# ScalarE multiplies more of a slot table's rows; three PSUM bank strings and the order of the first stage's steps change

## The chip, the cores and the metric

The kernel runs on one core of a Trainium2 chip. The metric is the device time of one execution in microseconds, the median of several runs. The engines of the core work side by side, each through its own queue in order: PE (TensorE: matmuls and transposes), ACT (ScalarE: activations and copies), DVE (VectorE), POOL (GpSimd) and SP (SyncE, which issues most of the DMAs). PE writes its results to PSUM, which here is eight banks of 128 x 512 f32. A bank can be written again only when the engine that reads it has read it.

## What is computed

The input x is 8 batches of 512 tokens with 512 features. Two branches read the same layernorm of it, and their product is added to x:

```python
xn = _layernorm(x, axis=-1)
s = _L0_attn_ref(xn, Wq, Wk, Wv, Wo, Wg1, Wg2, norm_weight)
g = _silu(_L0_ffn_ref(xn, gate_w, Wg, Wu, Wd, sWg, sWu, sWd, shared_gate_w))
x = x + s * g
```

The first branch is linear attention with a decay, 16 heads of 32, in chunks of 128 tokens:

```python
q = silu(xn @ Wq); k = silu(xn @ Wk); v = xn @ Wv        # by heads
q, k = rotate(q), rotate(k)
scores = einsum('bthd,bshd->bhts', qi, ki) * D           # in a chunk
o_inter = einsum('bthd,bhde->bthe', qi * decay_q, S)     # the chunks before
S = lam_C * S + einsum('bshd,bshe->bhde', ki * decay_k, vi)
o = group_rmsnorm((o_intra + o_inter) * sigmoid(xn @ Wg1 @ Wg2)) * norm_weight
s = o @ Wo
```

The second is a mixture of 16 experts (512 to 128 to 512, SwiGLU). The router picks four of them for each of the 4096 tokens and scales their softmax weights to a sum of one. A shared expert, the same for all tokens, is added under a sigmoid gate.

## The kernel before

**Stages.** By the trace: to about 200 us the first stage, in which every batch is normed, transposed, routed and sent through the shared expert, a piece at a time (`first`, a generator), between the parts of batch 0's attention. From 200 to 226 the tokens are sorted by expert (`sort`) while PE ends batch 0's attention. From 226 to 284 the slot table is made (`table`), between the parts of batch 1's attention. From 304 to 693 the expert blocks run over gathered tokens, at full PE. From 693 on come the attention of batches 2 to 7 and the mixture of all parts into the output.

**PSUM.** `bank(tag, name)` (L115) gives one of four rings: "a" of four banks, "k" and "m" of one each, "d" of two. Keys (`key`, a product with wk and then Silu on ACT, L669) take "m", queries "d". The values (`value`, L615, copied by ACT at L619) take "m" for even tiles and "d" for odd ones. Scores (`scores`, L725) take all four of "a", which DVE empties by multiplying with a mask (L750). The state products (L714) lie in "k".

**The first stage's pieces for a batch**, in order: route_1 (plT, "a"), share_1 (pg in "m", read by Silu, and pu in "d"), then norm of a later batch and turn of the next (psT, four transposes to "a", copied by ACT at L291), route_2 (pl, a transpose to "a"), and share_2, whose four row tiles pys_b_t take the banks of a string, are copied by ACT (L374) and stored. Names in the trace carry the batch and tile: pys_2_0 is batch 2's first row tile. The stores and loads of x, the two halves of xn_d (L262, L275) and xT_d go through SP's queue. `along` is the step that `sequence(0, ...)` calls: each call runs one or two such pieces (nine fifths on average).

**A group of four heads** in `sequence(b, step, ...)`: scores of group g, a step, the key product of group g + 2 (or a value tile of the next batch, where there is no such group), the transpose of the next group's keys (by_token, L691, then ACT's kd at L696), a step, the query of g + 2, the output (po, L766 and L772, multiplied into on by DVE, L776), a step. Behind the first group's query stands the second half of the gate (gate_2, tiles p at L645), four "a" banks read by ACT's Sigmoid into on (L649). gate_2 runs at this place for batches 0 and 1 only. For batch 0 the step is `along`. For batch 1 it does nothing, and the table's parts are called from within products instead (between[0], after each of the four matmuls).

**The slot table.** `sort` has given each of the 128 lists (a rank and a tile of tokens) its places. The lists are taken in eight groups of 16 (GROUP). For a group, make(i) writes two one-hot arrays in two halves of eight lists each: place (L526, 128x512 f16) and block (L529, 128x2288 f16). The row of a list in place is then multiplied by the tokens' numbers: for the first eight lists of a group by one DVE instruction (L533, with half_token), for the other eight by number(), one ACT instruction for each list (L542, 128x64 f16). Sixteen matmuls (pn, L565, an "a" bank) multiply place with block, and DVE adds the result up (L574; the first is a cast, L576). Two homes for place and block alternate between groups. number(i + GROUP, ...) is called in three parts, of lists 0 to 4, 5 to 9 and 10 to 15, the first before and the others behind the matmuls of group i.

**Order.** Each engine's order is fixed when the kernel is built. Matmuls are issued in the order of the program; the instructions of ACT and DVE stand in their queues as a scheduler of the build has placed them.

Of the kernel before, what the change touches and what calls it, by code (L numbers as in the profile page):

```python
# [47 lines left out]
GROUP = 16  # L48
# [49 lines left out]
def tile_block(ctx: ExitStack, tc: tile.TileContext, a: dict, out: bass.AP):  # L98
# [8 lines left out]
    def bank(tag, name):  # L107
        return pp.tile([P, 512], F32, tag=tag, name=name, bufs={"a": 4, "k": 1, "m": 1, "d": 2}[tag])
# [255 lines left out]
    def share_2(b):  # L364
        h = h1_of.pop(b)
        xT1_of.pop(b)
        for t in range(NC):
            sh = p1.tile([P, D], F32, tag="sh1", name=f"sh1_{b}_{t}", bufs=6)
            py = bank("dama"[t], f"pys_{b}_{t}")
            with on_pe():  # L370
                nc.tensor.matmul(
                    py, lhsT=h[:, t * P : (t + 1) * P], rhs=sw[:, KC * 2 * F :],
                    start=True, stop=True)
            nc.scalar.copy(sh, py)  # L374
            nc.sync.dma_start(sh_d[b][t * P : (t + 1) * P, :], sh)
# [110 lines left out]
    def table(room):  # L486

        half = room.bitcast(F16)  # L490
        free = [0]
        quads = GROUP // QUAD


        def part(*shape):
            n = int(np.prod(shape))
            free[0] += n
            flat = half[:, free[0] - n : free[0]]
            return flat.rearrange("p (q j) -> p q j", j=QUAD) if len(shape) == 2 else (
                flat.rearrange("p (u q j) -> p u q j", u=quads, j=QUAD))  # L500

        homes = [(part(quads, HALF, QUAD), part(quads, 2 * NB, QUAD))]
        free[0] = 2 * WE * (LATE - LATE // 2)
        homes.append((part(quads, HALF, QUAD), part(quads, 2 * NB, QUAD)))

        def flat(n):
            free[0] += n
            return half[:, free[0] - n : free[0]]

        acc = flat(2 * NB)  # L510

        def rows(of, n):
            return of.rearrange("p (u j) -> p u j", j=QUAD).unsqueeze(2).to_broadcast(
                [P, of.shape[-1] // QUAD, n, QUAD])

        def make(i):
            place, block = homes[i // GROUP % 2]
            for u in range(0, quads, quads // 2):
                us = slice(u, u + quads // 2)
                lists = slice(i + u * QUAD, i + (u + quads // 2) * QUAD)  # L520

                def counts(n):
                    return count[:, :n].unsqueeze(1).to_broadcast([P, quads // 2, n, QUAD])

                with tc.issue_after(masked[0]) if i == GROUP and u == 0 else nullcontext():
                    nc.vector.tensor_tensor(  # L526
                        place[:, us], counts(HALF), rows(sp[:, 0, lists], HALF), ALU.is_equal)
                with tc.issue_after(masked[0]) if i == GROUP and u == 0 else nullcontext():
                    nc.vector.tensor_tensor(  # L529
                        block[:, us], counts(2 * NB), rows(sp[:, 1, lists], 2 * NB),  # L530
                        ALU.is_equal)
                if u == 0:
                    nc.vector.tensor_tensor(  # L533
                        place[:, us], place[:, us], rows(half_token[:, lists.start % NT :][
                            :, : GROUP // 2], HALF), ALU.mult)

        def number(i, some):
            place = homes[i // GROUP % 2][0]
            for j in range(max(some[0], GROUP // 2), some[1]):
                row = place[:, j // QUAD, :, j % QUAD]  # L540
                t = (i + j) % NT
                nc.scalar.activation(row, row, AF.Copy, scale=token[:, t : t + 1])  # L542

        yield
        make(0)
        for j in range(0, GROUP, 4):
            number(0, (j, j + 4))
            yield
        for i in range(0, TOPK * NT, GROUP):
            more = i + GROUP < TOPK * NT  # L550
            if more:
                make(i + GROUP)
            else:
                for e in range(E - LATE, E - LATE // 2):
                    nc.sync.dma_start(wexp[:, e, :], a["experts"][:, e, :])
            if i < TOPK * NT // 2:
                yield
            place, block = homes[i // GROUP % 2]
            pn = bank("a", f"pn_{i}")
            for some in ((0, 5), (5, 10), (10, GROUP)):  # L560
                if some[0] == 5:
                    with on_pe():
                        for j in range(GROUP):
                            h = j % 2 * HALF
                            nc.tensor.matmul(  # L565
                                pn[h : h + HALF, : 2 * NB],
                                lhsT=place[:, j // QUAD, :, j % QUAD],
                                rhs=block[:, j // QUAD, :, j % QUAD], start=(j < 2),
                                stop=(j >= GROUP - 2))
                if more:  # L570
                    number(i + GROUP, some)
                if some[1] == GROUP:
                    if i:
                        nc.vector.tensor_tensor(acc, acc, pn[:, : 2 * NB], ALU.add)  # L574
                    else:
                        nc.vector.tensor_copy(acc, pn[:, : 2 * NB])  # L576
                yield
        pt = bank("a", "pslot")
        with on_pe():
            for h in range(2):  # L580
                nc.tensor.matmul(
                    pt[h * HALF : (h + 1) * HALF, :NB], lhsT=fold,
                    rhs=acc.rearrange("p (b h) -> p b h", h=2)[:, :, h], start=True, stop=True)
        t = const.tile([P, NB], I32, tag="slot", name="slot")
        with behind(DVE):
            nc.vector.tensor_scalar(t, pt[:, :NB], float(B * N // 2), None, ALU.add)
        slots.append(t)
# [90 lines left out]
    def key(b, g, ps=None):  # L678
        kT_of[g] = rotated(b, g, "k", wk, ps)
# [177 lines left out]
    def sequence(b, step, projected, before=None, defer=False, also=lambda: None):  # L857


        n = b + 1  # L860

        def project_tiles(q, ts):
            if q is not None:
                for t in ts:
                    projected(q, t, project(q, t))


        fill = ([0], [1], [2], [3], [], [], [], [])
        for g in range(G):
            scores(b, g)  # L870
            step()
            if g + 2 < G:
                key(b, g + 2)
            else:
                value(n, 2 * (g - 2))
            if g + 1 < G:
                by_token(b, g + 1)
            project_tiles(before, fill[2 * g])
            step()
            if g + 2 < G:  # L880
                query(b, g + 2)
                if g + 3 == G and n not in xT_of:
                    load_xT(n)
            if g + 2 == G:
                value(n, 1)
            if g == 0 and b not in on_of:
                gate_2(b)
            project_tiles(before, fill[2 * g + 1])
            if fill[2 * g + 1] == [NC - 1]:
                on_of.pop(before, None)  # L890
            output(b, g)
            if defer and g + 2 == G:
                gate_1(n)
            step()
        v_of.pop(b)
        if n == FIRST:
            for _ in range(4):
                next(filling)
            gate_1(n)
            next(filling, None)  # L900
            for e in range(E - LATE // 2, E):
                nc.sync.dma_start(wexp[:, e, :], a["experts"][:, e, :])
            squares(b)
            inverse(b)
            value(n, 3)
            normed(b)
            experts_of_blocks()
            return
        if defer:
            gate_2(n)  # L910
        value(n, 3)
        also()
        squares(b)
        step()
        inverse(b)
        key(n, 0)
        also()
        query(n, 0)
        normed(b)
        also()  # L920
        if not defer:
            step()
        key(n, 1)
        by_token(n, 0)
        if defer:
            step()
        query(n, 1)
        also()
        if not defer:
            gate_1(n)  # L930
            project_tiles(b, [0, 1])
            also()
            project_tiles(b, [2, 3])
            also()
            on_of.pop(b)
        step()
# [556 lines left out]
```

## Time and profile before

| | us |
|---|---|
| median of three runs | 1140.58 (1140.27 to 1141.29) |
| the profiled execution | 1134.81 |
| its span in the trace | 1133.0 |
| first stage, to about 200: PE busy | 188.72 of 200.00 |
| table, 226 to 284: PE, DVE, ACT busy | 53.57, 55.51, 30.81 of 58.00 |
| blocks, 304 to 693: PE busy | 389.00 of 389.00 |
| 693 to 1133: PE busy | 429.92 of 440.00 |

The span is the time from the first to the last instruction of the profiled execution; all places in the trace are given in microseconds from its start. A line of a timeline has the start, the duration of a run of like instructions, the engine, the line of the kernel, the operation, and out<-in. A remark in brackets gives the idle time of the engine before it and what ended it. A line of the list of waits has what waited, for what, and then the total, the number and the longest of such waits.

### The profile page before, as it was taken

To read this page: it belongs to the slowest core of one execution; us is meant where nothing else is said; L and a number is where in the kernel's file an instruction comes from. 1 tells how busy PE (TensorE), PEld (TensorE's weight loads), DVE (VectorE), ACT (ScalarE), POOL (GpSimd) and SP (SyncE) were. 2 spreads that over 40 slices of the span, in tenths; PEclk is the share of its full clock that TensorE was granted. 3 is DMA by queue.
4 is the path that set the end of the run, shared out by engine and by line. 5 is a ranking of instruction groups with operands and counts; after the bars stand their busy time and mean duration, and the time that the engine had idled before them with its cause. 6 is when DMAs were issued, how large, how long until landed. Compare 5 with 4: busy or idle time off the path is not lost. (4 is left out here: it accounts for less than half of the span.)

```text
span 1133.0 us, 21299 instructions
## 1 busy us (share of the span) xinstructions
PE 1106.5 (98%) x7670; PEld 675.5 (60%) x7670; DVE 737.3 (65%) x1584; ACT 428.6 (38%) x924; POOL 447.2 (39%) x430
## 2 busy tenths in 40 slices
PE   7999999998999999999999999999999999999998
PEld 4445554455577777777777775655645555546453
DVE  6357744899344455444445446968889597797774
ACT  3223424264443333333333442353442522523541
POOL 4212100200333333333333323855877858858211
PEclk9999999999999999999999999999999999999999
DMA  9995342092789999989999975824647537444012
GB/s 341 326 319 191 143 151 48 22 383 70 239 201 234 244 236 241 240 237 239 237 240 249 256 204 216 292 81 142 232 121 236 177 113 258 143 136 142 19 38 75
DMA packets 163930, 218.48 MB, mean 193 GB/s; under 512 B 89840, under 2 KB 99184, under 8 KB 161776
## 3 DMA queue, kind: packets, MB, share of 16 engines
q1 hardware_dynamic: 142704, 146.76, 41.6%
q0 software_dynamic: 21120, 70.34, 23.4%
q8 instruction: 63, 1.03, 0.4%
q14 instruction: 43, 0.35, 0.1%
HBM read 126.78 MB, written 72.43 MB: 176 GB/s over the span
## 5 line engine op out<-in xcount | busy, mean ns | idle before, releaser
L1224 PE MATMUL pgu<-xts,wst 128*128 128x256 f32 x896 | 202.6, 379 | 0.0
L1224 PEld LDWEIGHTS pgu<-xts,wst 128*128 128x128 f32 x896 | 170.1, 190 | 46.2 <-issue 13.2
L1343 POOL DMA_INDIRECT yg<-y_d,place x128 | 142.8, 1115 | 30.3 <-issue 18.3
L1153 POOL DMA_INDIRECT more<-xn_d,slot x69 | 65.6, 951 | 216.6 <-DVE w L1207 113.8
L1255 PE MATMUL py<-wexp,slb 128*128 x272 | 129.9, 593 | 0.0
L1259 DVE TENSOR_SCALAR y<-py,w 128x512 f32<-128x512 f32 x136 | 102.0, 750 | 41.5 <-PE py L1255 34.8
L615 PE MATMUL pv<-wv,xT 128*128 128x512 f32 x256 | 118.2, 602 | 1.0 <-ACT sh L374 1.0
L659 PE MATMUL pk<-xT,wk 128*128 128x512 f32 x256 | 118.2, 603 | 0.0
L659 PE MATMUL pq<-xT,wq 128*128 128x512 f32 x256 | 115.7, 593 | 0.3 <-PEq L1307 0.3
L1236 ACT ACTIVATE slb<-pgu 128x256 f32<-128x256 f32 (+1 forms) x80 | 28.2, 352 | 222.7 <-PE pgu L1224 180.6
L1237 DVE TENSOR_TENSOR slb<-slb,pgu 128x256 f32<-128x256 f32 (+1 forms) x80 | 30.5, 381 | 121.1 <-ACT slb L1236 121.1
L817 PE MATMUL pw<-wo,on 128*128 128x512 f32 x224 | 100.6, 596 | 5.2 <-DVE m L1381 4.4
L1153 POOL DMA_INDIRECT xg<-xn_d,slot x67 | 63.7, 950 | 101.4 <-DVE w L1207 48.2
L1385 POOL TENSOR_TENSOR xo<-xo,m 128x512 f32<-128x512 f32 x31 | 45.3, 1462 | 128.1 <-DVE m L1381 120.9
L1186 ACT COPY xts<-pl 128x512 uint16<-128x512 uint16 x110 | 84.3, 769 | 2.4 <-DMA pl<-more 1.3
L750 DVE TENSOR_TENSOR sc<-ps,dmask 128x512 f32<-128x512 f32 x128 | 79.0, 676 | 1.0 <-PE ps L725 1.0
L659 PEld LDWEIGHTS pq<-xT,wq 128*128 128x128 f32 x256 | 47.2, 190 | 54.2 <-issue 52.7
L615 PEld LDWEIGHTS pv<-wv,xT 128*128 128x128 f32 x256 | 46.0, 190 | 51.3 <-issue 46.8
L659 PEld LDWEIGHTS pk<-xT,wk 128*128 128x128 f32 x256 | 46.2, 189 | 50.7 <-issue 48.3
L817 PEld LDWEIGHTS pw<-wo,on 128*128 128x128 f32 x224 | 41.2, 190 | 54.5 <-issue 45.2
L1205 DVE COPY wst<-wexp 128x512 f32 x112 | 43.2, 426 | 37.0 <-DVE y L1259 15.7
L1255 PEld LDWEIGHTS py<-wexp,slb 128*128 128x128 f32 x272 | 45.5, 191 | 27.4 <-issue 26.8
(196 smaller groups left out, 1713.1 us busy)
## 6 DMA issues: line engine op xcount, KB each, us to landing
y_d<-y SPq DMA_DIRECT2D x136, 256.0 KB, 4.1
wexp<-in_experts SPq DMA_DIRECT2D x16, 768.0 KB, 5.0
sh_d<-sh SPq DMA_DIRECT2D x32, 256.0 KB, 3.5
xT<-xT_d SPq DMA_DIRECT2D x8, 1024.0 KB, 6.7
m<-sh_d SPq DMA_DIRECT2D x32, 256.0 KB, 4.6
xo<-in_x SPq DMA_DIRECT2D x32, 256.0 KB, 2.8
out<-xo SPq DMA_DIRECT2D x31, 256.0 KB, 2.0
x<-in_x SPq DMA_DIRECT2D x7, 1024.0 KB, 8.8
```

The lines of the kernel that those rows point to most:

```text
L615: nc.tensor.matmul(pv, lhsT=xT_of[b][:, k, t * P : (t + 1) * P], rhs=wv[:, k, :], start=(k == 0), stop=(k == KC - 1))
L659: nc.tensor.matmul(ps, lhsT=w[:, k, g * P : (g + 1) * P], rhs=xT_of[b][:, k, :], start=(k == 0), stop=(k == KC - 1))
L750: masked[:] = [nc.vector.tensor_tensor(s, pss[j].rearrange("p (c t) -> p c t", t=C), dmask[:, g * HG + j].unsqueeze(1).to_broadcast([P, NC ...
L817: nc.tensor.matmul(pw, lhsT=on_of[b][:, g, t * P : (t + 1) * P], rhs=wo[:, g, :], start=(g == 0), stop=(g == G - 1))
L1153: nc.gpsimd.indirect_dma_start(out=row(i), out_offset=None, in_=xn_d, in_offset=bass.IndirectOffsetOnAxis(ap=slot[:, i : i + 1], axis=0))
L1186: (nc.vector.tensor_copy if j in by_dve else nc.scalar.copy)(xt[:, u, KP:, :].bitcast(U16).rearrange("p k (t h) -> p h k t", h=2), pls[j % ...
L1205: nc.vector.tensor_copy(to, wflat[:, bass.ds(off + u * KC * F, KC * F)])
L1224: nc.tensor.matmul(pg[:, o * 2 * P : (o + 1) * 2 * P], lhsT=wst[j % 2][k // KP][:, (k % KP * 2 + o) * F :][:, :F], rhs=xt[:, :, k, :], sta ...
L1255: nc.tensor.matmul(py, lhsT=hT[:, u * P : (u + 1) * P], rhs=wflat[:, bass.ds(off + KC * 2 * F, D)], start=True, stop=True)
L1259: gone.append(nc.vector.tensor_scalar(y, py, w[:, u : u + 1], None, ALU.mult).ins)
L1343: nc.gpsimd.indirect_dma_start(out=yg, out_offset=None, in_=y_d, in_offset=bass.IndirectOffsetOnAxis(ap=place[:, r, g : g + 1], axis=0))
L1385: nc.gpsimd.tensor_tensor(xo, xo, m, ALU.add)
```

## The change

- In make(), L533 is now issued for the first half of group 0 alone, and not for each group. In number(), the rows start from list 0 for all groups but the first. So seven DVE instructions of 128x512 go, and 7 x 8 = 56 ACT instructions of 128x64 come.
- share_2 takes the banks "mdaa" for its four row tiles in place of "dama", for all eight batches.
- In sequence, for batch 0, the step behind the scores now stands behind the key product (or value tile). For other batches it stays where it was.
- gate_2 at batch 1's first group takes "aaam", so that its last tile lies in the key's bank. For batch 0 it stays "aaaa".

```diff
@@ share_2
-            py = bank("dama"[t], f"pys_{b}_{t}")
+            py = bank("mdaa"[t], f"pys_{b}_{t}")
@@ table: make, number
-                if u == 0:
+                if i == u == 0:
                     nc.vector.tensor_tensor(
                         place[:, us], place[:, us], rows(half_token[:, lists.start % NT :][
                             :, : GROUP // 2], HALF), ALU.mult)
 
         def number(i, some):
             place = homes[i // GROUP % 2][0]
-            for j in range(max(some[0], GROUP // 2), some[1]):
+            for j in range(max(some[0], 0 if i else GROUP // 2), some[1]):
                 row = place[:, j // QUAD, :, j % QUAD]
                 t = (i + j) % NT
                 nc.scalar.activation(row, row, AF.Copy, scale=token[:, t : t + 1])
@@ sequence
             scores(b, g)
-            step()
+            if b:
+                step()
             if g + 2 < G:
                 key(b, g + 2)
             else:
                 value(n, 2 * (g - 2))
+            if not b:
+                step()
             if g + 1 < G:
                 by_token(b, g + 1)
...
             if g == 0 and b not in on_of:
-                gate_2(b)
+                gate_2(b, banks="aaam" if b else "aaaa")
```

No matmul, no load and no store is added or left out.

## The prediction

> **What bounds the kernel now.** I read the busy shares first, then busy time by stage, then PE's waits, then the timeline of each place where PE waits.
>
> ```profile
> PE 1106.5 (98%) x7670; PEld 675.5 (60%) x7670; DVE 737.3 (65%) x1584; ACT 428.6 (38%) x924; POOL 447.2 (39%) x430
> ```
>
> PE is busy for 1106.5 of 1133.0 us, so a gain can only come from its waits or its work, and its work stays as it was. By stage (PE, PEld, DVE, ACT, POOL, clock, DMA share, GB/s):
>
> ```profile
> 200.00:226.00 26.00, 26.00 (x122) 12.17 (x121) 23.74 (x44) 4.76 (x11) 5.95 (x5) 1.00 0.07 19
> 226.00:284.00 58.00, 53.57 (x730) 31.59 (x732) 55.51 (x103) 30.81 (x97) 0.00 (x0) 1.00 0.61 229
> 304.00:693.00 389.00, 389.00 (x1697) 289.50 (x1695) 187.21 (x478) 153.18 (x301) 123.04 (x130) 1.00 0.92 231
> ```
>
> The slot table is made at 226 to 284, beside batch 1: there DVE is full (55.51 of 58) and PE waits for it. From 304 to 693 PE never pauses, so whatever PE gains or loses earlier is handed on to the end. PE's waits up to 335 us (total, times, longest):
>
> ```profile
> PE psT L289 <- DVE mv L252: 6.9, 1, 6.9
> PE pn L565 <- DVE sc L750: 3.1, 2, 2.3
> PE p L645 <- DVE wexp L576: 1.4, 1, 1.4
> PE psT L289 <- DVE sc L750: 1.0, 1, 1.0
> PE pv L615 <- ACT sh L374: 1.0, 1, 1.0
> PE pg L355 <- ACT sh L374: 0.9, 1, 0.9
> PE pl L318 <- DVE sc L750: 0.8, 1, 0.8
> ```
>
> The 6.9 is the start-up. The others are all that the change can win: some 3.7 us in the first stage, 4.5 in the table stage.
>
> **First stage, what goes.** Listed waits run from a modelled end; the true cost is the start less the start that the order alone would give, which lies 0.1 to 0.17 earlier. pg_2 starts at 55.49, not 54.50: 0.99. psT at 154.97, not 153.86: 1.11. pl_7 at 180.06, not 179.23: 0.83. pv_2 at 184.86, not 183.65: 1.21. Sum 4.14. pg_2 and pv_2 wait because the third shared row tile, before them in the one bank "m", must be copied by ACT; psT and pl_7 wait for scores' "a" banks, which DVE empties by L750, and the step after key or value puts 3.5 us of PE work between. I take all four as gone.
>
> **First stage, what comes.** "m" has one buffer. Each pair of its users that the new order makes adjacent on PE pays a turnaround. The waits show the price:
>
> ```profile
> 184.24 1.06 ACT L374 COPY sh<-pys 128x512 f32<-128x512 f32 x2
> 184.86 1.55 PE L615 MATMUL pv<-wv,xT 128*128 128x512 f32 x3 [1.04 <-ACT sh L374]
> ```
>
> The first copy takes 0.59 (184.24 to 184.83) and PE starts 0.03 later. And in the kernel before, pys_2_0 follows pk_0 at once, because it takes a "d":
>
> ```profile
> 64.32 3.60 PE L659 MATMUL pk<-xT,wk 128*128 128x512 f32 x8
> 67.76 1.45 PE L371 MATMUL pys<-sw,h 128*128 128x512 f32 x3
> 67.96 0.60 ACT L669 ACTIVATE sk<-pk 128x512 f32<-128x512 f32 x1 [2.73 <-PE pk L659]
> ```
>
> With "mdaa" it needs pk_0's own bank: Silu 67.96 + 0.60 + 0.03 = 68.59, not 67.76: 0.83. Reading the new banks along PE's built order I find five such pairs: pk_0 then pys_2_0, pk_2 then pg_4, pk_3 then pg_5 at 0.83 each; pv_2 of batch 0 then pys_1_0 (46.5 us) and pv_2 then pys_7_0 at 0.72, where a transpose (pl, 0.11) lies between. Sum 3.93. Net: 3.93 - 4.14 = -0.2.
>
> **What else the steps' move touches.** On PE it puts pk_2, pk_3, pv_0 and pv_2 ahead of a step each. pv_0 now starts at 153.9 and needs xT_1; its load is issued at 143.55 on SP's queue and lands in 6.7 (median), at 150.3: 3.6 spare, and SP's built order has it earlier, ahead of four stores of hs. SP's other swaps (xn_d stores against loads of x) lie before 100 us, with DMA full; I cost them at nothing since x is loaded steps ahead, and at 0 to 1.0 for the range, by the 1.04 that pv waited. POOL's queue is unchanged. pl_7 now comes behind pv_2: PE at 182.8, the mask's DVE chain from lg to L345 takes 2.9 as before (181.72 to 184.62), so it is ready at 186.1, and ptotal comes at 187.1: cover shrinks from 3.8 to 1.0, and if it goes, ptotal waits for the excess.
>
> **Table stage, what goes and comes.** Seven of eight L533 multiplications leave DVE (0.42 long, 0.34 start to start): 7 x 0.34 = 2.4 at most. ACT takes 56 more L542 rows. Their price by a row: eight back to back in 2.04, 0.24 each, so 13.5 us; by the mean of a single one, 0.353, it is 19.8. I take 0.24, since they come in runs of 5 to 11. The Trainium skill's "VectorE: DVE Perf Modes", section "TRN2 errata — SBUF-src ops pay a fixed extra latency per instruction", says a small SBUF tile pays a fixed bubble, 224 cycles on ScalarE, and to prefer tiles of 512 elements or more. For 64 elements at 1.2 GHz it gives 0.240 as an estimate, the row's step; it speaks against trading 7 wide DVE instructions for 56 narrow ones.
>
> ACT has the time (30.81 + 13.5 of 58), but its queue is in order, and the new rows stand ahead of things PE and DVE wait for:
>
> ```profile
> 237.49 0.60 ACT L669 ACTIVATE sq<-pq 128x512 f32<-128x512 f32 x1 [3.60 <-PE pq L659]
> 238.10 1.28 ACT L649 ACT_TABLE_LOAD   x1
> 240.39 2.07 ACT L649 ACTIVATE on<-p 128x512 f32<-128x512 f32 x4 [1.00 <-PE p L645]
> ```
>
> In the built order five rows stand ahead of sk_2, eight ahead of sq_2, ten between sq_2 and the table load. Following it from 230 us in before's times:
> - The five rows need group 1's first place (L526, 232.83 + 0.42, ready to ACT at 233.29), so sk_2 runs at 234.49 to 235.09, not 232.37; DVE's L671, free at 234.42 without L533, waits 0.71.
> - Group 2's place is ready at 238.1; five rows end at 239.3, sq_2 at 239.9, ten more at 242.3, the table load at 243.6. The four sigmoids (on) run at 243.6 to 245.7, not 240.4 to 242.5.
> - PE's gate matmuls no longer wait for L576 (2.05 by the start). But ps_1 needs the "a" banks that on reads, and "aaam" gives it only the fourth: it starts at 245.25, not 242.47, and pk_3, which needs the fourth's "m", at 246.3:
>
> ```profile
> 242.47 1.19 PE L725 MATMUL ps<-qT,kT 32*128 32x128 f32 x32
> 243.59 2.84 PE L659 MATMUL pk<-xT,wk 128*128 128x512 f32 x6
> ```
>
> - There PE is 2.7 behind. DVE, at L776, waits 1.26 for on; its next place operation waits 0.84 for PE's pn_16; L671 of sk_3 0.15. With the 0.71, DVE waits 2.96 and has saved 6 x 0.34 = 2.04 by then.
> - PE's later waits (pn_48, 0.8; pn_80, 2.3) take most of the 2.7 back: pn_48's goes, pn_80's falls to 1.55. sc_3 ends at 276.95, not 275.91, and pn_112 starts 1.0 later.
>
> Table stage: +1.0. The Trainium skill's "ScalarE: Activation LUTs", section "What ACT_TABLE_LOAD costs", puts a table switch at about 2.66 us with a drain. Here the load takes 1.28 and the next row can follow at once; by the page each of the two loads would put on back by 1.4, and the sum would be +2.4. I go by the row.
>
> Sum: -0.2 + 1.0 = +0.8, all of it passed on at 304: the span 1133.0 becomes 1133.8. The profiled run took 1134.81 and the runs' median is 1140.58, 7.6 above the span; I keep that: 1141.4.
>
> **Rivals.**
> 1. Faster, because ACT keeps up: sk, sq and on come so early against their readers that nothing waits for them, and the 2.4 of DVE time comes off the stage that DVE fills. For it: DVE 55.51 of 58. Against: the chain above, where sk, sq and on each come 2 to 3 us later. -0.2 - 2.4: 1138.0. If also the turnarounds were hidden, -4.14 - 2.4: 1134.0, but nothing on PE lies in those gaps.
> 2. Slower, by one mechanism: on is late and PE's 2.7 at ps_1 isn't won back, because DVE, itself 1 us late, stays the last for pn_80 and sc_3. It decides if pn_80's wait stays at 2.3. Then -0.2 + 2.7 = +2.5: 1143.1; with rows of 0.353, the 23 ahead of on add 23 x 0.11 = 2.6 more: 1145.7. For it: DVE has 2.5 us free in 58. Against: the two waits are on the page.
> 3. The turnarounds alone: as the forecast, but the table stage neutral: 1140.4. It falls within the same band.
>
> **Numbers.** 0.2%, or 2.3 us, is about what a measurement of this kernel can tell from no change: 1138.3 to 1142.9. Forecast with rival 3: 0.52; rival 2: 0.30; rival 1: 0.18. The forecast's own range is 1139.9 to 1142.9 (each stage to 0.8 or so). The range of 8 in 10 takes in rival 1's 1138.0 and most of rival 2, of which it leaves out the end with the dear rows: 1137.8 to 1144.8. Faster 0.18, same 0.52, slower 0.30.
>
> **What would show it.** Right, if PE's list loses pg, psT and pl behind L374 and L750 before 200, and shows five waits of 0.6 to 0.7 by the list for ACT (sk L669, v L619); if on runs some 3 us later against the start of its batch, ps L725 waits for it (about 2.7), and pn's waits shrink. Wrong, if pys and pg start without waiting after pk, if L542's step isn't near 0.24, or if the stretch 226 to 284 holds less PE idle time than 4.4. A change of pace after 304 would mean that I missed a cause altogether.

## The result and the profile after

The changed kernel takes 1142.07 us (median of 12 runs) where the kernel before, run beside it, takes 1138.85: a ratio of 1.0035 (95% interval 1.0023 to 1.0047), slower, and by more than the 0.2% that the forecast took as no change. The forecast's time, 1141.4, is only 0.7 us off, but by luck: it rested on 1140.58 as the time before, 1.7 above the median here, and on a loss of 0.8 us. The loss is 3.2 us by the medians and 4.0 by the ratio.

The busy shares of the changed kernel, and its stages (PE, PEld, DVE, ACT, POOL, clock, DMA share, GB/s):

```profile
PE 1110.8 (98%) x7670; PEld 677.5 (59%) x7670; DVE 738.9 (65%) x1577; ACT 441.2 (39%) x980; POOL 447.0 (39%) x430
```

```profile
200.00:226.00 26.00, 26.00 (x122) 12.17 (x121) 22.73 (x44) 5.28 (x12) 5.94 (x5) 1.00 0.04 14
226.00:284.00 58.00, 53.08 (x595) 29.84 (x595) 51.92 (x93) 38.82 (x139) 0.00 (x0) 0.94 0.56 210
...
304.00:693.00 389.00, 389.00 (x1697) 289.64 (x1695) 187.08 (x485) 154.05 (x302) 124.35 (x132) 1.00 0.94 232
```

DVE did lose work in the table stage and ACT got it. The fixed stretch shows this only roughly, since the table ends later in the changed kernel; over the whole table (227.48 to 283.32 before, 228.69 to 288.93 after) DVE's busy time went from 53.73 to 51.90 us and ACT's from 29.82 to 43.00. PE lost 0.5 us of busy time between 226 and 284, though, and the column before the DMA share differs: the granted clock was 0.94 there, and 1.00 before and after. The blocks are full as before, so nothing was won back. PE's waits:

```profile
PE psT L289 <- DVE mv L252: 7.0, 1, 7.0
PE ps L725 <- ACT on L649: 3.3, 1, 3.3
PE pg L355 <- ACT sk L669: 2.8, 2, 2.0
PE pn L565 <- DVE sc L750: 1.6, 2, 1.4
PE pys L371 <- ACT v L619: 1.1, 2, 0.6
PE pw L817 <- DVE on L810: 0.8, 1, 0.8
PE pys L371 <- ACT sk L669: 0.7, 1, 0.7
```

The four waits of the first stage that the change was to remove are gone, and so is p's for L576. In their place stand pys and pg behind ACT, and one wait of 3.3 us at ps L725.

To compare profiles of different executions I take three places on PE: the first pu matmul (16.13 us in the kernel before; it differs by the start-up), batch 1's first scores (227.48) and pslot, the end of the table (283.32). The first stage is the time from the first to the second, 211.35 us before, and the table from the second to the third, 55.84. The changed kernel has 1.16 more in the first stage and 4.40 more in the table. Kernels whose first stage is as before show -0.13 to -0.15 there, so 0.14 is the play of the start, and the first stage's loss is 1.3.

**First stage.** PE and ACT of the changed kernel around pg_5, the shared product behind pk_3:

```profile
124.84 3.70 PE L659 MATMUL pk<-xT,wk 128*128 128x512 f32 x8
130.57 3.70 PE L355 MATMUL pg<-xT,sw 128*128 128x512 f32 x8 [2.03 <-ACT sk L669]
```

```profile
128.62 1.28 ACT L669 ACT_TABLE_LOAD   x1 [4.92 <-PE pk L659]
129.92 0.60 ACT L669 ACTIVATE sk<-pk 128x512 f32<-128x512 f32 x1
```

pk_3 ends at 128.5. sk_3 is the first Silu after batch 0's sigmoids, so a table load stands ahead of it, and it begins only when pk_3 is there: 1.28, then Silu's 0.60, then pg_5 at 130.57, 0.05 after Silu's end. The turnaround is 2.1 us by the starts, not 0.83. In the kernel before, the first Silu after the sigmoids was sl_5, beside pu_5's matmuls, and its load had ended 3.6 us before pg_5 was there, so it cost PE nothing:

```profile
122.02 1.28 ACT L359 ACT_TABLE_LOAD   x1
126.88 0.60 ACT L359 ACTIVATE sl<-pg 128x512 f32<-128x512 f32 x1 [3.57 <-PE pg L355]
```

ACT stood idle for 4.92 us ahead of sk_3's load too, but this load began only when pk_3 was there, in all six profiles with this order of steps. Why one load runs ahead of its Silu's input and the other doesn't, the runs don't show.

**Table.** ACT, PE and the clock in the changed kernel (columns of the last as above):

```profile
240.51 0.58 ACT L669 ACTIVATE sq<-pq 128x512 f32<-128x512 f32 x1
240.99 2.50 ACT L542 ACTIVATE wexp<-wexp,token 128x64 f16<-128x64 f16 x10
243.51 1.28 ACT L649 ACT_TABLE_LOAD   x1
244.80 2.06 ACT L649 ACTIVATE on<-p 128x512 f32<-128x512 f32 x4
```

```profile
241.65 0.48 PE L725 MATMUL ps<-qT,kT 32*128 32x128 f32 x2
245.45 3.05 PE L725 MATMUL ps<-qT,kT 32*128 32x128 f32 x30 [3.32 <-ACT on L649]
248.43 5.12 PE L659 MATMUL pk<-xT,wk 128*128 128x512 f32 x6
```

```profile
240.00:244.00 4.00, 2.13 (x78) 1.70 (x70) 4.00 (x8) 3.98 (x15) 0.00 (x0) 1.00 1.02 424
244.00:248.00 4.00, 2.54 (x29) 2.16 (x30) 2.58 (x7) 3.11 (x6) 0.00 (x0) 0.78 1.01 418
248.00:252.00 4.00, 4.00 (x10) 1.72 (x6) 2.48 (x4) 0.00 (x0) 0.00 (x0) 0.50 1.00 357
252.00:256.00 4.00, 4.00 (x25) 2.01 (x24) 1.77 (x3) 1.25 (x5) 0.00 (x0) 0.87 1.05 405
```

Ten rows of L542 and the table load run between sq_2 and the sigmoids (on). PE is through with batch 1's first output early, issues two of the next 32 scores matmuls, and waits 3.32 us. Then it gets on, but soon at half speed: from 246.2 to 253.0 the clock is 0.50. The other scores matmuls take 3.05 us (all of them took 1.19 before; at full clock, in e3 below, these take 2.13, since on's four tiles come one by one), and pk_3's six take 5.12, not 2.84. In finer slices the half clock lasts 6.83 us.

### The profile page after: what moved, and what is told of

Read it like the earlier page. It is cut to its first block, busy times and chain, and to the rows that moved or that the text cites. A ratio compares the mean times of both kernels' runs of the same rounds, so it can differ in the third digit from the quotient of the medians.

```text
span 1138.7 us, 21375 instructions
## 1 busy us (share of the span) xinstructions
PE 1110.8 (98%) x7670; PEld 677.5 (59%) x7670; DVE 738.9 (65%) x1577; ACT 441.2 (39%) x980; POOL 447.0 (39%) x430
## 5 line engine op out<-in xcount | busy, mean ns | idle before, releaser
L659 PE MATMUL pk<-xT,wk 128*128 128x512 f32 x256 | 120.7, 614 | 0.0
L734 ACT COPY blocked<-state 32x96 f32<-32x96 f32 x96 | 30.7, 320 | 82.1 <-DVE state L729 81.2
```

What stands on the lines that cost most here:

```text
L659: nc.tensor.matmul(ps, lhsT=w[:, k, g * P : (g + 1) * P], rhs=xT_of[b][:, k, :], start=(k == 0), stop=(k == KC - 1))
```

## The experiments

e1 to e4 ran on a chip (the first, below) on which the kernel before takes 1150.97 us (35 runs); e5 to e8 ran on a second, beside 1139.39 (28 runs), and e9 to e11 on a third, beside 1139.11 (23 runs). Ratios are to the kernel before on the same chip. The columns in the middle are profiles against the profile of before, in us, by the places above, with the half clock that fell in each.

| run | first stage | table | half clock in them | ratio (95%) |
|---|---|---|---|---|
| the change | +1.16 | +4.40 | 6.83 in the table | 1.0035 (1.0023 to 1.0047) |
| e5, the change again | +1.09 | +3.66 | 6.82 in the table | 1.0030 (1.0015 to 1.0045) |
| e1, first stage only | +1.07 | +2.55 | 3.41 and 3.41 in the table | 1.0032 (1.0011 to 1.0053) |
| e2, rows and gate | -0.15 | +3.43 | 6.83 in the table | 1.0019 (0.9999 to 1.0038) |
| e3, change, PE kept busy | +1.08 | +1.23 | none | 1.0030 (1.0011 to 1.0049) |
| e6, e3 again | +2.78 | +1.24 | 3.41 in the first stage | 1.0011 (0.9997 to 1.0025) |
| e8, rows, gate as before | -0.14 | +1.75 | 3.41 in the table | 1.0021 (1.0004 to 1.0037) |
| e9, gate only | -0.13 | +1.68 | 3.42 in the table | 1.0005 (0.9995 to 1.0015) |
| e4, "dmaa", step behind values | -4.74 | 0.00 | none | 0.9961 (0.9938 to 0.9983) |
| e11, "dmaa", step behind all | -1.44 | -0.01 | none | 1.0000 (0.9987 to 1.0012) |
| e7, e4 and late rows | -4.75 | -0.87 | none | 0.9936 (0.9919 to 0.9954) |
| e10, e7 and gate | -4.75 | -0.88 | none | 0.9936 (0.9921 to 0.9950) |

### The parts apart: e1 and e2

e1 keeps, of the diff, only "mdaa" and the steps; e2 only the rows and the gate's "aaam".

> Only the banks "mdaa" and the first stage's steps; the table and the gate as before. Theory A (the result is two losses that add: 1.2 us in the first stage, mostly the turnarounds plus a table load ahead of sk_3's Silu, and 4.4 us at the slot table, 3.4 of it a halved TensorE clock after a PE pause of 3.3 us): scores of batch 1 start 1.2 us later than before, no half clock, +1.2 us at the end. Theory B (the first stage's loss is only there because the profile before was a good one, or it is absorbed): 0 at the end. My prediction's step for this part said -0.2.

> Only ScalarE's rows (all groups but the first) and the gate's "aaam"; banks and steps of the first stage as before. Theory A: the whole pause and the half clock are here, +4.4 us, granted clock 0.5 for some 6.8 us after ps_1's wait. Theory B (the lateness of batch 1 against the sort, by the first stage, is needed for the pause): pause under 3 us, no half clock, +1.0 us.

The first stage's loss is in e1 as in the whole (+1.07), and none of it in e2. The pause of 3.3 us and the 6.83 us of half clock are in e2 (+3.43), so batch 1 need not be late for them. Each loss lies where theory A puts it, though e2's is 3.43 and not 4.4, and e2's time alone can't be told from no change. Theory A's "no half clock" for e1 failed: the rows there are those of before, and so are the waits (1.37 at p, 2.31 at pn_80), yet after each of the two the clock was halved for 3.41 us, and the table took 2.55 longer. By the times e1 loses as much as the whole change (1.0032).

### Is it the clock? e3 and e6

```diff
         pss = [bank("a", f"ps_{b}_{g}_{j}") for j in range(HG)]
+        if b == 1 and g == 1:
+            with on_pe():
+                for _ in range(3):
+                    nc.tensor.matmul(
+                        pss[0], lhsT=wk[:, 0, :P], rhs=xT_of[b][:, 0, :], start=True, stop=True)
```

The three matmuls' results are overwritten by the scores.

> The changed kernel, with three extra matmuls of 128x512 (2.65 us of PE time, at 0.44 each half) into ps_1_0's bank just ahead of batch 1's second scores, which overwrite it: PE is busy in most of its pause, and no other engine does anything else. Theory A (a pause of 3.3 us makes the clock drop, and the clock is the loss): no half clock, ps_1 and pk_3 at full speed, 3.4 us faster than the changed kernel, +2.2 us against the kernel before. Theory B (DVE and ACT are the bound there, and half clock hides in their waits): the clock stays full but the end does not move, +4 to +5.7 us against before.

> The changed kernel itself, again, beside the next three on one chip. Against the kernel before: 1.0023 to 1.0047 times, as in the result. In its profile the half clock stands after ps_1's wait (6.8 us long), and the gather of the slot table (pslot) comes 5.6 us later than in the profile of before. If the half clock is chance, its place or length differs from the first profile.

> The changed kernel with three extra matmuls in PE's pause, again, now beside the changed kernel on the same chip. Theory A (the clock is 3.2 us of the loss): granted clock higher in the mean of the runs, pslot 3.2 us earlier than in the changed kernel, and the time 2 to 3.2 us shorter. Theory B (the first such run was luck of the clock): clock and time as in the changed kernel.

PE and clock of e3, whose lines from the scores on are numbered five higher than the changed kernel's:

```profile
241.59 2.84 PE L723 MATMUL ps<-xT,wk 128*128 128x512 f32 x6
244.36 0.48 PE L730 MATMUL ps<-qT,kT 32*128 32x128 f32 x2
245.43 2.13 PE L730 MATMUL ps<-qT,kT 32*128 32x128 f32 x30 [0.58 <-ACT on L649]
247.49 2.84 PE L659 MATMUL pk<-xT,wk 128*128 128x512 f32 x6
```

```profile
244.00:248.00 4.00, 3.41 (x35) 2.14 (x34) 2.86 (x8) 3.08 (x6) 0.00 (x0) 1.00 1.02 417
248.00:252.00 4.00, 4.00 (x24) 1.94 (x23) 3.10 (x6) 0.47 (x2) 0.00 (x0) 1.00 1.00 408
```

The extra matmuls (ps<-xT,wk) run from 241.59 to 244.4, on is still late, and the wait left at ps is 0.58. The clock stays at 1.00 and pk_3 takes 2.84 again. The table is then 1.23 us longer than before, against 4.40: 3.2 us were the clock's, about half of 6.83, by a kernel that does more work. e6 repeats it: +1.24. But e5, the change on e6's chip, has +3.66, so there the clock's part is 2.4 us, and by e2's +3.43 it would be 2.2. The half clock is as long in all three. In the change it begins at 246.22, when PE is at work again (245.45); in e5 it begins at 245.42 and in e2 at 242.93, before the pause ends (246.19 and 244.15), and what lies in the pause slows nothing: pk_3's six take 5.12, 4.35 and 4.13. The first stage of e6 shows the same toll elsewhere, behind pg_5's wait:

```profile
130.63 5.40 PE L355 MATMUL pg<-xT,sw 128*128 128x512 f32 x8 [2.03 <-ACT sk L669]
```

```profile
130.00:132.00 2.00, 1.37 (x2) 0.73 (x3) 1.38 (x4) 0.58 (x1) 0.00 (x0) 0.69 0.00 0
132.00:136.00 4.00, 4.00 (x8) 1.60 (x7) 1.20 (x2) 0.00 (x0) 0.00 (x0) 0.73 0.00 0
240.00:256.00 16.00, 15.39 (x182) 9.04 (x182) 13.91 (x25) 10.42 (x29) 0.00 (x0) 1.00 1.01 407
```

Half of its 3.41 us is the 1.70 by which its first stage is longer than e3's. Over all runs of that chip the mean granted clock was 0.9977 for the kernel before, 0.9961 for the change and 0.9980 for e6; times two and the span, that is 5.2, 8.9 and 4.6 us at half clock. e6 is 2.85 us faster than e5 by the medians (1139.74 against 1142.59), within the 2 to 3.2 expected (2.2 by the ratios, whose intervals overlap). Its pslot comes 0.7 us earlier than e5's, not 3.2: 2.4 are won in the table and 1.7 lost in the first stage. On the first chip e3's time alone (+3.5 us by the median) would not have told the theories apart: runs scatter there by 10 us, and the half clock averages 11.6 us in the kernel before.

### The gate's bank: e8 and e9

e8 is e2 with "aaaa" for batch 1; e9 is the kernel before with "aaam".

> ScalarE's rows alone; the gate keeps four "a" banks in batch 1 as well, the first stage is as before. It tells what "aaam" is worth. Theory A (ps_1 needs three of the four banks that on reads, or four): ps_1's first matmul waits for all of on, the pause grows from 3.3 to 3.8 us, pk_3 starts no later than ps_1 ends; the table's end is 0 to +0.6 us against the rows with "aaam" (pslot +3.3 against before). Theory B (the first scores tile that "aaam" lets go ahead splits the pause and saves a drop of the clock, or causes one): a change of 3 us either way.

> Only the gate's "aaam" in batch 1; nothing else changed. Theory A (the fourth gate tile waits for L576 because it takes the bank of pn's first group; with "m" it need not): PE's wait of 1.4 us at p goes, on is read out some 1.4 us earlier, and DVE, which is full there, takes part of it back at pn_48 and pn_80: pslot 0 to 1.4 us earlier, -0 to -1.4. Theory B (the wait only moves to ps_1, as in the changed kernel): a wait of 1 to 2 us at ps L725 for on, pslot within 0.3.

In e8 the fourth gate tile still needs pn_0's bank, so p waits 1.7 us for L576, and none of the listed waits is at ps: the pause is not longer, as theory A had it, but broken in two (ps takes 2.51 us at full clock instead of 1.19). The clock was halved for 3.41 us, not 6.83, and the table is 1.7 us shorter than with "aaam" in e2: theory B's kind of change, at half its size. By the times the two can't be told apart. In e9 p doesn't wait:

```profile
241.41 2.30 PE L725 MATMUL ps<-qT,kT 32*128 32x128 f32 x32
...
246.97 1.22 PE L565 MATMUL pn<-wexp 128*64 128x286 f16 x16 [0.49 <-DVE sc L750]
```

But its scores take 2.30 us instead of 1.19, which fits waits for on, tile by tile, and pn_16 (246.97) and pn_48 (1.16) wait longer for sc, DVE being no faster. The table's +1.68 is the half clock's (3.42 / 2 = 1.7), which came behind pn_80's wait, as in e1:

```profile
275.25 1.23 PE L565 MATMUL pn<-wexp 128*64 128x286 f16 x16 [2.31 <-DVE sc L750]
276.41 4.51 PE L615 MATMUL pv<-wv,xT 128*128 128x512 f32 x6
```

So "aaam" alone is worth nothing (1.0005), and theory B is right that the wait only moves, though no wait at ps is listed and the half clock makes pslot later than its 0.3. Beside late on it moves into one long pause.

### Without the turnarounds: e4 and e11

```diff
-            py = bank("dama"[t], f"pys_{b}_{t}")
+            py = bank("dmaa"[t], f"pys_{b}_{t}")
...
-            step()
+            if b or g + 2 < G:
+                step()
             if g + 2 < G:
                 key(b, g + 2)
             else:
                 value(n, 2 * (g - 2))
+            if not (b or g + 2 < G):
+                step()
```

That is e4; e11 has the change's own condition (the step behind keys and values).

> The kernel before, with "dmaa" for the shared rows (m at the second tile) and the first stage's step behind the value tiles only (groups 2 and 3), not behind the keys. Theory A (the four waits of the first stage are each a late reader of a bank, and the new turnarounds come from m being the first tile and pg following pk): all four waits go and no turnaround comes, -4.1 us. Theory B (the waits only move, since DVE or the sort is as late as PE): between -1 and +1 us.

> The kernel before with "dmaa" and the first stage's step behind key and value tiles alike, as in the change. Against the one with the step behind value tiles only (pslot 4.3 us earlier than before): theory A (pg_4 waits for sk_2, 0.75, and pg_5 for sk_3 and the table load ahead of it, 2.03, listed; some 2.9 by the starts): 1.4 us earlier than before in the profile of the sort (ptotal), so the keys' steps cost 2.9; 1.7 more if the clock is halved after pg_5's wait. Theory B (the turnarounds at the keys hide something else that the value-only kernel pays): more than 2.5 us earlier than before.

PE's waits of e4:

```profile
PE psT L289 <- DVE st L250: 6.5, 1, 6.5
PE pn L565 <- DVE sc L750: 3.1, 2, 2.3
PE py L1258 <- DVE slb L1240: 1.5, 1, 1.5
PE p L645 <- DVE wexp L576: 1.4, 1, 1.4
PE pw L817 <- DVE on L810: 0.8, 1, 0.8
PE psT L289 <- DVE x L242: 0.2, 1, 0.2
```

All four waits are gone, and no new one stands in the first stage (py's 1.5 lies in the blocks, and in all four profiles of that chip). A row tile takes 0.9 us (3.60 for four), longer than a turnaround, and the second tile has one of them ahead of it and two behind; the keys keep a whole step between themselves and pg. -4.74 by the profile (-4.6 with the play of the start) and 0.9961 by the times; theory A. With the steps behind the keys too, e11 gives 3.3 of it back (2.9 expected by theory A), most of it at pg_4 and pg_5, whose waits for sk are 2.8 in its list as in the change's. By its time it is as fast as the kernel before (1.0000): the 1.4 us of its profile are at the edge of the interval, and its mean half clock, 6.1 us against 4.6, takes back some 0.8 of them.

### Rows where nothing waits for them: e7 and e10

```diff
-                if u == 0:
+                if u == 0 and (i < 4 * GROUP):
...
-            for j in range(max(some[0], GROUP // 2), some[1]):
+            for j in range(max(some[0], GROUP // 2 if i < 4 * GROUP else 0), some[1]):
```

on top of e4; e10 adds "aaam".

> The kernel before with "dmaa", the step behind the value tiles only, and ScalarE's rows for groups 4 to 7 only, where no Silu, sigmoid or table load stands behind them in ScalarE's queue. Theory A (rows cost when they stand ahead of sk, sq and on; DVE's time is worth something where PE waits for sc: pn_80, 2.3 us): -4.3 for the first stage and up to 4 x 0.34 = -1.4 more at pn_80, -5 to -5.7 in all. Theory B (the rows delay the value copies and pn just as much): -4.3 to -3.

> "dmaa", the step behind the value tiles only, ScalarE's rows for groups 4 to 7 only, and the gate's "aaam". Against the same without "aaam" (-7.5 us by the runs, pslot 5.0 us earlier): theory A, 0.5 to 1.4 us faster, with no wait over 1 us at p or ps_1; theory B, the same within 0.3 us.

PE's waits of e7 in the table:

```profile
PE pn L565 <- DVE sc L750: 2.2, 2, 1.4
PE p L645 <- DVE wexp L576: 1.4, 1, 1.4
```

pn's longest wait fell from 2.3 to 1.4, the table is 0.87 shorter, and in the first stage e4's gain stands. e7 takes 1131.91 us against 1139.39 (0.9936), e10 1131.96 against 1139.11: the best of all, and faster than both kernels. e10 is theory B, the same. The two ratios rest on 6 and 5 runs. The profiles account for 5.6 of e7's 7.3 us by the ratio; that is within the interval (5.2 to 9.2 us), and what the rest is was not settled.

## Why the prediction was right or wrong

- **First stage, what goes: right.** The four waits were priced at 4.14; e4, which removes them and adds nothing, gains 4.6.
- **First stage, what comes: one term was mis-sized.** Of the five turnarounds, the four others appear as worked out (pys behind v and sk, and pg_4, wait 0.6 to 0.8 by the list). pg_5's was priced like them, 0.83, by the Silu alone. It is 2.1, because the step took sk_3 past sl_5 and with it the table load: 1.28 more. With it the sum is +1.1 in place of -0.2; measured +1.3.
- **The later covers held.** pv_0 had its xT_1, and ptotal its mask: neither waits in the changed kernel.
- **ACT's rows: right.** They take 0.25 each (ten in 2.50), sk_2, sq_2 and on come as late as the replay had them, and pn_80's wait fell to 1.45 (1.55 forecast). The table's loss without the half clock is 1.23, forecast 1.0.
- **The table load itself: the row was right.** on begins 0.01 us behind the load's 1.28. The drain that the Trainium skill's "ScalarE: Activation LUTs", section "What ACT_TABLE_LOAD costs", adds to each switch doesn't show.
- **What failed is the step "There PE is 2.7 behind".** It took PE's time at ps_1 as a lag to be won back at pn_48 and pn_80. But removing p's wait turned two waits into one pause of 3.3 us, and behind it the clock was halved for 6.83 us. This cost 3.2 us (2.4 in e5, 2.2 in e2) which the sum doesn't have, though the pause was in its own numbers (245.25 less 242.47 - 2.05, or 4.8; by the starts 3.8 came). The profile of before has no half clock anywhere before PE's end, so no row there priced it. The Trainium skill's "TensorE: Matmul & The Clock Gate", section "Why this matters for your kernels", warns of PE gaps above some 3 us, which bring the clock down to half; the 3.32 us here did so in each of the three profiles that had it.
- **The rivals.** "Slower" came, but not by rival 2's mechanism: it needed pn_80's wait to stay at 2.3. Rival 1 is excluded by e2 and e8: the rows as placed don't gain. In another place, groups 4 to 7, they gain 0.87. Rival 3's neutral table is out too: it is 1.2 longer in e3 and e6, without any half clock in it.

The account of the change by the runs on the second chip: 1.3 for the first stage, 1.2 for the table's waits, and (8.9 - 5.2) / 2 = 1.9 for the clock in the mean of the runs, 4.4 together; measured 1.0030 (1.7 to 5.1 us). The account isn't tight: for e3 on the first chip, whose mean half clock is 8.7 us against 11.6, it gives 1.3 + 1.2 - 1.5 = 1.0 us, and 3.5 (1.3 to 5.6) was measured; what the rest is stays open. The spans of the two profiles differ by more, 5.7, because the profiled execution of before had no half clock at all, which is rare: two of that kernel's 28 runs on the second chip show a mean clock of 1.000.

## What to carry to other kernels

When a change makes two short pauses of PE into a long one, price the clock as well as the pause: 3.3 us of waiting cost 2.2 to 3.2 us more behind it. When an activation is moved ahead of another, see which of them now carries the table load, and who waits for it. In a ring of one bank, choose for each user a place with other work on both sides: "dmaa" and the step behind the values gave 4.6 us where "mdaa" and the step behind all lost 1.3.

## What the hardware showed that was not expected

Every half clock while PE had work lasted 3.41 to 3.42 or 6.82 to 6.83 us, on all chips. The Trainium skill's "TensorE: Matmul & The Clock Gate", section "What's actually happening", tells of a free-running window of 3413 ns, which these lengths fit: one window or two. Pauses well under 3 us were enough for one window, in some executions and not in others: 1.37 and 2.31 us in e1, 1.7 in e8, 2.31 in e9, 2.03 in e6, while the profile of before has 1.36 and 2.31 in the same places at full clock. The traces show why the same pause can be hit in one execution and not in another. Within a profile the changes of the clock lie whole windows apart: e1's four half clocks begin 34.13, 631.47 and 78.50 us after one another, which is 10, 185 and 23 times 3.413. So each profile can be cut at its windows' edges. The 2.31 us ahead of pn_80 are then split between two windows in the kernel before (the first two rows), and fall into one window in e9 (the third row), behind which the clock is halved:

```profile
270.00:273.41 3.41, 1.95 (x34) 1.10 (x31) 3.38 (x9) 2.04 (x8) 0.00 (x0) 1.00 0.00 0
273.41:276.82 3.41, 2.57 (x20) 1.61 (x20) 3.41 (x8) 0.00 (x0) 0.00 (x0) 1.00 0.02 5
...
272.97:276.38 3.41, 1.13 (x16) 0.93 (x16) 3.37 (x10) 0.83 (x4) 0.00 (x0) 1.00 0.00 0
276.38:279.79 3.41, 3.41 (x6) 1.51 (x5) 3.41 (x8) 0.00 (x0) 0.00 (x0) 0.50 0.03 5
```

Over the 13 profiles, up to 1125 us, there are 13 windows at full clock in which PE idles for 1.9 us or more, and 12 of them are followed by half clock. Of 34 with 1.2 to 1.9 us 3 are, and of some 4200 with less 4, all four on the first chip. So it is the idle time in one window that counts, more than the length of a pause; what sets off the seven others is open, and no run here puts a pause at a chosen place of the window. This makes a time of this kernel scatter by several microseconds, and a single profile can hold a half clock that another execution of the same kernel hasn't.
